# Out projection of later token tiles in groups of four with two levels of Winograd products, and where the residual stream is transposed

## The chip, the cores and the metric

The kernel runs on one core of one Trainium2 chip. The metric is the device time of one execution in microseconds (us). An execution that the hardware profiler records gives a span, from the first to the last instruction, and the device time around it. The engines are called PE (matrix products; PEld is its weight load), DVE (vector), ACT (scalar and activation), POOL (GpSimd) and SP (which here only issues DMAs). PE reads SBUF and writes PSUM; ACT and DVE read either.

## The reference, cut to what matters

Two residual blocks over 4096 tokens (64 batches of 64) of width 1024. All of it is f32 until the feed forward rounds to bf16.

```python
def reference(x, itok_B_0_15, itok_B_0_7, ...):
    # 1: a per-batch 64x64 matrix over channels, attention with 32 heads of 32, out projection
    x = x + _L0_attn_ref(_L0_cond_ref(x, itok_B_0_15, L0_cond_weights), qkvw, qkvb, ow, ob)
    # 2: dense layer with routed low-rank experts, then a quantized gated feed forward
    x = x + _L0_ffn_ref(_L0_cond2_ref(x, itok_B_0_7, W, Wr, A, B), w_gate, s_wgate, ...)
    return x
...
    def _L0_attn_ref(x, attn_qkvw, attn_qkvb, attn_ow, attn_ob):
        ...
        ctx = jnp.einsum('bhqk,bhkd->bhqd', probs, v)
        ctx = jnp.transpose(ctx, (0, 2, 1, 3)).reshape(B, S, H)
        return ctx @ attn_ow + attn_ob
```

The change is to the last line, `ctx @ attn_ow + attn_ob` and the sum with x, and to how its result, the residual stream x1, gets to the second block.

## The kernel before, in words

4096 tokens are 32 tiles of 128 rows; two tiles are a pair, so there are 16 pairs. The instructions of each engine stand in the order in which the code emits them. A tile pool hands out SBUF; a tile that takes the place of an older one waits for all uses of the older one (`reuse_waits="tile"`), whichever engine or DMA they are on.

**Attention** (`attention`) works on eight blocks of 512 tokens and writes its context, transposed, to DRAM (`ctx_d`, one tensor per pair). In the tail of the last block pairs 0 and 1 of out projection fill PE.

**Products in Winograd's form.** `Winograd` (its `product` is at L1129) computes a 256x1024 by 1024x1024 product from four quarters of each operand with seven products of quarters in place of eight. ORDER = (1, 6, 7, 5, 2, 4, 3) is the order, A_OF and B_OF name the weight and token operand of each. Four PSUM banks (`poa` to `pod`) are each used for two or more of the seven; a later product goes on summing in a bank that has been read. The weight operands A11, A12, A22 are quarters of the weight and S1 to S4 sums of quarters, made once early in the kernel and held in DRAM (`comb`). The token operands T1 to T4 are made on DVE by `sums_of_tokens` (L1139 to L1142), the context being the stationary operand and the weights the moving one (512 columns).

**Out projection** (`OutProjection`). `pair(p)` gives seven pairs of functions, `product` and `rest`. Before the first product POOL adds the bias to the two x tiles (L1250, 1024 columns each). `rest` of 1 copies the bank on ACT (`u1`, L1261), of 6 and 7 adds it on DVE to the sum before (`u6`, `u7`, L1263), and after 7 POOL adds u6 and u7 to three quarters of x (L1266, 512 columns). `rest` of 5, 2, 4 and 3 adds the bank on DVE to its quarter of x (L1269).

**The residual stream's transpose.** The second stage needs x1 with its features on the partitions. `turn` splits a half row of x1 on ACT into its low and high 16-bit planes (L1224, `xh`, 1.04 us each), has SP issue a DMA transpose of them (L1226, `xhT`), and `turned` joins the planes on ACT (L1235, `xTo`, 1.34 us each) and stores f32 to `xT_d`. That is four times per pair. SP also stores x1 itself to `out_t`, loads the context and x of the pair after next, and the second stage's base weights (one of seven per pair).

**The second stage** (`second_stage`) first runs pairs 2 to 15 of out projection, then its own 16 pairs, the last written out by hand. Three pairs are in flight (p, q = p-1, r = p-2): router and base product of p (seven products by `Winograd`, with the experts' part added in the banks), quantization and gate and up products of q, down product and result of r. `load_x1` brings the transposed x1 of the next pair (L1317), `token_sums` makes T1 to T4, `quant_a` and `quant_b` go DVE, ACT, DVE, then a DMA transpose on SP (`qT`, L1575), which the `pg` and `pu` matmuls (L1589) wait for.

## Time and profile before

| | |
|---|---|
| median of 3 runs (lowest, highest) | 2402.47 us (2402.36, 2408.15) |
| the profiled execution | 2406.19 us |
| its span, 41907 instructions | 2404.4 us |
| mean granted PE clock | 0.997 |
| out projection, pairs 2 to 15 | until 1712.0 us, where the first router matmul starts |
| second stage | 1712.0 us to the end |
| PE in it, steady state | a pair every 41.7 us (router matmuls at 1907.68 and 1949.42) |

Columns that recur below: in the groups of the page, `line engine op out<-in shapes xcount | busy us, mean ns of one | idle us before it, and what ended it`; in the timeline, `start us, length us, engine line op out<-in shapes xcount [idle before it <-releaser]`. Instructions of one engine are pipelined, so a recorded length can overlap the next start; the distance from start to start is what one costs when many stand in a row. A matmul of f32 operands leaves two records.

In out projection the slice view of the page shows PE at nine tenths or more and the DMAs at seven to eight tenths:

```profile
PE   8999999999999999999999999999999999999997
...
DVE  3573474464543644633535533324377878777787
ACT  1344344343344443443434544343333333333333
POOL 4121112111122223220000333334100000000000
PEclk9999999999999999999999999999999999999999
DMA  7899799899899998997967788877733443444353
```

Each digit is a fortieth of the span, 60.1 us; out projection ends in the 29th.

### The profile page before, as it was taken

Reading aid. Unit: us, or ns where it says so; the run is one execution under the profiler, and the core shown is the slowest. Engines: PE = TensorE matmul, PEld = TensorE weight load, DVE = VectorE, ACT = ScalarE, POOL = GpSimd, SP = SyncE. Lnnn points to the kernel's source line nnn. Section 1 sums busy time; section 2 is a strip of 40 time slices with the busy share of each in tenths; the row PEclk is TensorE's granted clock in tenths of the full one; section 3 lists DMA queues with packets and bytes.
Section 4 is the critical chain, followed back from the end, with each engine's and each line's share of the span. In section 5 each row is a group of like instructions: output and inputs, shape, how many; then the busy total and the mean of one; then the engine's idle time right before and its main releaser. Section 6 shows DMA issues by size and latency. Waiting matters only on the chain.

```text
span 2404.4 us, 41907 instructions
## 1 busy us (share of the span) xinstructions
PE 2367.6 (98%) x17066; PEld 1628.5 (68%) x17104; DVE 1334.5 (56%) x2584; ACT 936.2 (39%) x1220; POOL 418.7 (17%) x470
## 2 busy tenths in 40 slices
PE   8999999999999999999999999999999999999997
PEld 7888888888888888888888444444454545454452
DVE  3573474464543644633535533324377878777787
ACT  1344344343344443443434544343333333333333
POOL 4121112111122223220000333334100000000000
PEclk9999999999999999999999999999999999999999
DMA  7899799899899998997967788877733443444353
GB/s 229 217 240 248 190 228 241 221 232 220 208 232 274 212 255 230 242 237 179 207 188 196 213 257 258 275 218 248 239 77 75 90 79 83 84 86 82 70 119 76
DMA packets 612395, 453.84 MB, mean 189 GB/s; under 512 B 362465, under 2 KB 524258, under 8 KB 606690
## 3 DMA queue, kind: packets, MB, share of 16 engines
q1 hardware_dynamic: 581522, 393.91, 63.2%
q0 software_dynamic: 12240, 40.38, 7.9%
q10 hardware_dynamic: 18432, 16.79, 3.1%
q8 instruction: 137, 2.24, 0.4%
q14 instruction: 64, 0.52, 0.1%
HBM read 274.02 MB, written 91.23 MB: 152 GB/s over the span
## 4 chain that ended last, share of the span: by engine, by line
PE 92%; DMA 2%; DVE 1%; SPq 1%; issue 1%; ACT 0%; ACTq 0%; DVEq 0%
PE poa L1129 5%; PE poc L1129 5%; PE pod L1129 5%; PE psvc L530 4%; PE psva L530 4%; PE psvd L530 4%; PE pbc L1129 4%; PE pbd L1129 4%; PE pba L1129 4%; PE pskc L509 4%; PE pskd L509 4%; PE pska L509 4%; PE psqa L509 4%; PE psqd L509 4%; PE psqc L509 4%; PE pr L1398 2%
## 5 line engine op out<-in xcount | busy, mean ns | idle before, releaser
L582 ACT ACTIVATE prob<-prob 128x512 f32<-128x512 f32 x128 | 80.6, 629 | 346.7 <-DVE prob L578 338.6
L608 ACT COPY pT<-phT 128x1024 int16<-128x1024 int16 x128 | 165.4, 1339 | 25.4 <-DMA phT<-ph 21.4
L596 ACT COPY ph<-prob 128x1024 int16<-128x1024 int16 x128 | 133.5, 1043 | 63.1 <-DVE prob L590 38.4
L442 POOL COPY yB<-yhT 128x512 int16<-128x512 int16 (+1 forms) x84 | 75.8, 955 | 426.4 <-DMA yhT<-yh 426.4
L1636 POOL DMA_DIRECT2D out_dram<-y x29 | 25.2, 869 | 656.2 <-DVE y L1628 644.4
L577 DVE TENSOR_REDUCE mx<-s 128x8 f32<-128x512 f32 x128 | 87.4, 682 | 71.6 <-PE s L568 71.6
L1250 POOL TENSOR_TENSOR xo<-xo,ob 128x1024 f32<-128x1024 f32 x32 | 83.5, 2629 | 228.2 <-DVE prob L578 189.5
L509 PE MATMUL psqa<-yB,wq 128*128 128x256 f32 x512 | 121.1, 379 | 0.5 <-ACT psqp L479 0.5
L509 PE MATMUL pska<-yB,wk 128*128 128x256 f32 x512 | 120.9, 379 | 0.0
L1224 ACT COPY xh<-xo 128x1024 int16<-128x1024 int16 x64 | 64.4, 1041 | 142.8 <-DVE xo L1269 142.8
L530 PE MATMUL psva<-wv,yB 128*128 128x256 f32 x512 | 115.8, 379 | 0.0
L1129 PE MATMUL poa<-woA,cx 128*128 128x512 f32 x256 | 115.3, 593 | 0.0
L1129 PE MATMUL pba<-wtA,x1T 128*128 128x512 f32 x240 | 107.9, 592 | 0.0
L1235 ACT COPY xTo<-xhT 128x1024 int16<-128x1024 int16 x64 | 84.7, 1337 | 58.4 <-DMA xhT<-xh 53.3
L530 PEld LDWEIGHTS psva<-wv,yB 128*128 128x128 f32 x512 | 97.2, 190 | 14.0 <-issue 0.8
L509 PEld LDWEIGHTS psqa<-yB,wq 128*128 128x128 f32 x512 | 97.1, 190 | 14.0 <-ACT psqp L479 0.9
L509 PEld LDWEIGHTS pska<-yB,wk 128*128 128x128 f32 x512 | 97.3, 190 | 13.2
L633 ACT ACTIVATE co<-banks,bqkv 128x256 f32<-128x256 f32 x128 | 60.7, 474 | 109.3 <-PE banks L411 79.8
L1266 POOL TENSOR_TENSOR xo<-xo,ou 128x512 f32<-128x512 f32 x48 | 59.9, 1275 | 191.8 <-DVE ou L1263 191.8
L590 DVE TENSOR_TENSOR prob<-prob,den 128x512 f32<-128x512 f32 x128 | 89.4, 699 | 4.4
L578 DVE TENSOR_TENSOR prob<-s,mx 128x512 f32<-128x512 f32 x128 | 88.5, 691 | 4.5
L1129 PEld LDWEIGHTS poa<-woA,cx 128*128 128x128 f32 x256 | 48.5, 190 | 60.0 <-issue 59.5
(255 smaller groups left out, 4945.8 us busy)
## 6 DMA issues: line engine op xcount, KB each, us to landing
wv<-v_d SPq DMA_DIRECT2D x56, 512.0 KB
wq<-q_d SPq DMA_DIRECT2D x28, 1024.0 KB
wk<-k_d SPq DMA_DIRECT2D x28, 1024.0 KB
wq<-in_qkvw_dram SPq DMA_DIRECT2D x100, 256.0 KB
wk<-in_qkvw_dram SPq DMA_DIRECT2D x100, 256.0 KB
wv<-in_qkvw_dram SPq DMA_DIRECT2D x50, 512.0 KB
x<-in_x_dram SPq DMA_DIRECT2D x32, 512.0 KB
ctx_d<-co ACTq DMA_DIRECT2D x128, 128.0 KB
```

The source lines that it names most:

```text
L442: nc.gpsimd.tensor_copy(dst, src[:, :, :, halves[r] if hf else r])
L509: nc.tensor.matmul(ps[:, 0:HB], A[:, SLOT[A_OF[i]], k, :], B[B_OF[i]][:, k, :], start=first and k == 0, stop=k == KQ - 1, skip_group_check ...
L530: nc.tensor.matmul(ps[:, j * VC:(j + 1) * VC], B[B_OF[i]][:, k, j * P:(j + 1) * P], A[:, k, :], start=first and j == 0 and k == 0, stop=k ...
L577: nc.vector.tensor_reduce(mx, ps[:, :, n, :, :], AX.X, ALU.max)
L578: nc.vector.tensor_tensor(p.rearrange("p j h k -> p h j k"), ps[:, :, n, :, :], mx.unsqueeze(3).to_broadcast([P, HPC, 2, C]), ALU.subtract,)
L582: nc.scalar.activation(p, p, AF.Exp, scale=scale)
L590: nc.vector.tensor_tensor(p, p, den.unsqueeze(2).to_broadcast([P, n, C]), ALU.mult)
L596: nc.scalar.copy(h, planes(p.rearrange("p n k -> p (n k)")))
L608: nc.scalar.copy(planes(pT.rearrange("p a b q -> p (a b q)")), hT)
L1129: self.nc.tensor.matmul(ps, self.B[self.B_OF[i]][:, k, :], self.A[self.A_OF[i]][:, k, :], start=first and k == 0, stop=k == self.KQ - 1, s ...
L1235: nc.scalar.copy(planes(xT.rearrange("p k q -> p (k q)")), hT)
L1250: nc.gpsimd.tensor_add(s["x"][:, t, :], s["x"][:, t, :], self.ob)
```

## The change

Three things change together.

1. Pairs 4 to 15 become six groups of four token tiles (`OutGroups`). Each of the seven products of a group's Winograd form (the outer product) is itself computed in that form from seven products of quarters: 49 per group, each two matmuls with 256 moving columns. The second level's weight sums (S1, S2, S3 in new tiles, S4 in place of one quarter of the first level's operand) are made by DVE and POOL under pairs 2 and 3. For each outer product DVE makes four operand sums of 256 columns. Its seven products use three banks: `a` for 1, 6, 7 and 4, `b` for 5 and 3, `c` for 2. ACT copies (snapshots) bank `a` after 1, 6 and 7, into tiles with two buffers; POOL adds the snapshots, DVE adds banks `b`, `c` and the last of `a`. Each sum goes to U1, to U7 or to a quarter of x, as the first level needs, and POOL adds U1 or U7 to further quarters (`extra`). PE runs products 3 and 4 of the outer product before among those of the current one (`SEQ`). The bias is folded into U1 and U7.
2. x1's planes are stored to DRAM untransposed (`x1_d`), four plane copies on ACT per pair as before; the DMA transposes (`turned_x1`) and the joins of the planes (`joined_x1`, ACT) move into the second stage, two and two per pair, one pair ahead.
3. The second stage's base weights are loaded into the tiles of out projection's weights as each becomes free in the last group, rather than through the whole of out projection. The last pair's residual tiles are loaded as halves, the second tile's later.

The diff, cut to its core:

```diff
...
-    def turn(self, p, t):
+    def part(self, p, t):
 
         nc, n = self.tc.nc, self.H // 2
         for f in range(2):
             h = self.hp.tile([P, 2, n], I16, tag="h", name=f"xh_{p}_{t}_{f}")
             nc.scalar.copy(h, planes(self.st[p]["x"][:, t, f * n:(f + 1) * n]))
-            hT = self.hp.tile([P, 2, n], I16, tag="hT", name=f"xhT_{p}_{t}_{f}")
-            nc.sync.dma_start(
-                hT.rearrange("p h (k q) -> p (h k) q", q=P), h.rearrange("p h n -> p (h n)"), transpose=True
-            )
-            self.turning.append((p, t, f, hT))
-
-    def turned(self):
-        nc, n, KQ = self.tc.nc, self.H // 2, self.KC // 2
-        for p, t, f, hT in self.turning:
-            xT = self.hp.tile([P, KQ, P], F32, tag="xT", name=f"xTo_{p}_{t}_{f}")
-            nc.scalar.copy(planes(xT.rearrange("p k q -> p (k q)")), hT)
-            nc.sync.dma_start(self.xT_d[p][:, t, f * KQ:(f + 1) * KQ, :], xT)
-        self.turning = []
+            self.parted.append((self.x1_d[p][t, :, f, :, :], h))
+
+    def stored(self):
+        for to, h in self.parted:
+            self.tc.nc.sync.dma_start(to, h)
+        self.parted = []
 
...
+    SEQ = (("new", 1), ("old", 3), ("new", 5), ("new", 6), ("old", 4), ("new", 2), ("new", 7))
...
+    def open_right(self):
+        def pool(name, bufs):
+            return self.right.enter_context(self.tc.tile_pool(name=name, bufs=bufs, reuse_waits="tile", side="right"))
+        self.sp, self.tp, self.t2p, self.bp = pool("sg3", 1), pool("tg3", 1), pool("ug3", 2), pool("bg3", 5)
+
+    def open_left(self):
+        def pool(name, bufs):
+            return self.left.enter_context(self.tc.tile_pool(name=name, bufs=bufs, reuse_waits="tile"))
+        self.xp, self.up, self.snap = pool("xg3", 6), pool("vg3", 1), pool("ng3", 2)
+
...
+    def weight_sums(self, i):
+
+        nc, q = self.nc, self.QH
+        A = self.op.A[Winograd.A_OF[i]]
+
+        def a(m, h):
+            return A[:, 2 * h:2 * h + 2, m * q:(m + 1) * q]
+        S = self.sp.tile([P, 3, 2, q], F32, tag=f"S{i}", name=f"woS_{i}")
+        s1, s2, s3 = (S[:, n, :, :] for n in range(3))
+        self.W[i] = {"A11": a(0, 0), "A12": a(0, 1), "A22": a(1, 1), "S1": s1, "S2": s2, "S3": s3, "S4": a(1, 0)}
+        return [
+            lambda: nc.vector.tensor_tensor(s1, a(1, 0), a(1, 1), ALU.add),
+            lambda: nc.gpsimd.tensor_tensor(s3, a(0, 0), a(1, 0), ALU.subtract),
+            lambda: nc.vector.tensor_tensor(s2, s1, a(0, 0), ALU.subtract),
+        ], lambda: nc.vector.tensor_tensor(a(1, 0), a(0, 1), s2, ALU.subtract)
+
...
+    def operand_sums(self, o):
+
+        g, i = self.outers[o]
+        X = self.g[g]["B"][Winograd.B_OF[i]]
+        b = {f"B{h + 1}{t + 1}": X[:, 2 * h:2 * h + 2, t * P:(t + 1) * P] for h in range(2) for t in range(2)}
+        self.g[g]["b", i] = b
+
+        def sub(z, x, y):
+            b[z] = self.t2p.tile([P, 2, P], F32, tag=z, name=f"ug_{g}_{i}_{z}")
+            self.nc.vector.tensor_tensor(b[z], b[x], b[y], ALU.subtract)
+        return [
+            lambda: sub("T1", "B12", "B11"), lambda: sub("T2", "B22", "T1"), lambda: sub("T3", "B22", "B12"),
+            lambda: sub("T4", "B21", "T2"),
+        ]
+
...
+    def dests(self, g, i):
+
+        s = self.g[g]
+        if i in (5, 2, 4, 3):
+            T, N = {5: (1, 1), 2: (0, 0), 4: (0, 1), 3: (1, 0)}[i]
+            xd = (lambda t, n: self.x_unit(g, T, N, t, n),) * 2
+        ob = self.op.ob
+        U1 = lambda t, n: self.unit(s["U", 1], t, n)
+        return {
+            1: lambda: [(lambda t, n: ob[:, n * self.QH:(n + 1) * self.QH], U1)],
+            6: lambda: [(U1, U1)],
+            7: lambda: [(U1, lambda t, n: self.unit(s["U", 7], t, n))],
+            5: lambda: [(U1, U1), xd],
+        }.get(i, lambda: [xd])()
+
+    def add(self, o, unit, eng, what):
+
+        s, (g, i) = self.o[o], self.outers[o]
+        if i in (1, 7) and not s["begun"]:
+            self.g[g]["U", i] = self.up.tile([P, 2, self.HH], F32, tag=f"U{i}", name=f"vg_{g}_{i}")
+        for n, (src, dst) in enumerate(s["dests"]):
+            first = (n, unit) not in s["begun"]
+            s["begun"].add((n, unit))
+            eng.tensor_tensor(dst(*unit), what, (src if first else dst)(*unit), ALU.add)
+
+    def extra(self, g, i, unit):
+
+        s, gp = self.g[g], self.nc.gpsimd
+
+        def into(T, N, key):
+            x = self.x_unit(g, T, N, *unit)
+            gp.tensor_tensor(x, x, self.unit(s["U", key], *unit), ALU.add)
+
+        if i == 1:
+            into(0, 0, 1)
+        elif i == 7:
+            u = self.unit(s["U", 7], *unit)
+            c = self.HH + unit[1] * self.QH
+            gp.tensor_tensor(u, u, self.op.ob[:, c:c + self.QH], ALU.add)
+        elif i == 2:
+            into(1, 1, 7)
+        elif i == 4:
+            into(0, 1, 7)
+        elif i == 3:
+            into(1, 0, 1)
+
...
+    def product(self, o, j):
+        nc, (g, i) = self.nc, self.outers[o]
+        s = self.o[o]
+        bank = {1: "a", 6: "a", 7: "a", 4: "a", 5: "b", 3: "b", 2: "c"}[j]
+        first = bank not in s
+        if first:
+            pool, tag = (self.ps_c, "h") if bank == "c" else (self.ps_ab, "g")
+            s[bank] = pool.tile([P, 512], F32, tag=tag, name=f"pg{bank}_{g}_{i}")[:, 0:self.QH]
+        A, B = self.W[i][Winograd.A_OF[j]], self.g[g]["b", i][Winograd.B_OF[j]]
+        for k in range(2):
+            nc.tensor.matmul(
+                s[bank], B[:, k, :], A[:, k, :], start=first and k == 0, stop=k == 1, skip_group_check=True
+            )
+
+    def snapshot(self, o, j):
+        g, i = self.outers[o]
+        t = self.o[o]["s", j] = self.snap.tile([P, self.QH], F32, tag=f"s{j}", name=f"ng{j}_{g}_{i}")
+        self.nc.scalar.copy(t, self.o[o]["a"])
+
+    def after(self, o, j):
+
+        s, (g, i) = self.o[o], self.outers[o]
+        nc = self.nc
+        V, G = nc.vector, nc.gpsimd
+        if j in (1, 6, 7):
+            self.snapshot(o, j)
+        if j == 2:
+            self.add(o, (1, 0), G, s["s", 6])
+            self.add(o, (0, 0), V, s["c"])
+            self.add(o, (1, 1), V, s["b"])
+            self.add(o, (0, 0), G, s["s", 1])
+            self.extra(g, i, (0, 0))
+        elif j == 7:
+            self.add(o, (1, 1), G, s["s", 7])
+            self.extra(g, i, (1, 1))
+        elif j == 3:
+            self.add(o, (1, 0), V, s["b"])
+            self.extra(g, i, (1, 0))
+        elif j == 4:
+            self.add(o, (0, 1), V, s["a"])
+            self.extra(g, i, (0, 1))
+
...
+            for which, j in self.SEQ:
+                if which == "new" and not new or which == "old" and o == 0:
+                    continue
+                at = o if which == "new" else o - 1
+                self.product(at, j)
+                if j == 1:
+                    self.store()
+                self.after(at, j)
+                if j in (1, 6):
+                    self.part()
+                if new:
+                    if j in (1, 6) and sums:
+                        sums.pop(0)()
+                        if j == 1:
+                            sums.pop(0)()
+                    if j == 2 and sums:
+                        sums.pop(0)()
+                    if j == 2:
+                        if n == 0 and g != self.groups[0]:
+                            self.token_sum(g, 2)
+                        elif n == 2 and g != self.groups[0]:
+                            self.token_sum(g, 3)
+                        elif n == 5 and nxt:
+                            self.token_sum(nxt, 0)
+                        elif n == 6 and nxt:
+                            self.token_sum(nxt, 1)
+                    if j == 7 and n == 6 and nxt:
+                        for f in self.operand_sums(o + 1):
+                            f()
...
+        def turned_x1(p, *ns):
+
+            s = st1.setdefault(p, {"xT": {}})
+            for n in ns:
+                f, t = QUARTERS[n]
+                hT = s["hT", n] = op.hp.tile([P, 2, HH], I16, tag="h", name=f"x1h_{p}_{n}")
+                nc.sync.dma_start(
+                    hT.rearrange("p h (k q) -> p (h k) q", q=P), x1_d[p][t].rearrange("q f h n -> q f (h n)")[:, f, :],
+                    transpose=True,
+                )
+
+        def joined_x1(p, *ns):
+            s = st1[p]
+            for n in ns:
+                f, t = QUARTERS[n]
+                x = s["xT"][t, f] = xp1.tile([P, KQ, P], F32, tag="x", name=f"x1T_{p}_{n}")
+                nc.scalar.copy(planes(x.rearrange("p k q -> p (k q)")), s.pop(("hT", n)))
...
+        for p in (2, 3):
             for n, (_, product, rest) in enumerate(op.pair(p)):
                 product()
                 rest()
-            ld = next(loads_t, None)
-            if ld:
-                ld()
-            if p == NPAIR - 3:
+                for _ in range(2):
+                    if sums:
+                        sums.pop(0)()
+                if p == 2 and n >= 3:
+                    groups.load(g0, *((0, 1), (0, 0), (1, 1), (1, 0))[n - 3])
+                if p == 3:
+                    last_sums[Winograd.ORDER[n]]()
+                    if n in (1, 2, 3, 4):
+                        groups.token_sum(g0, n - 1)
+                    elif n > 4:
+                        for f in groups.operand_sums(0) if n == 5 else ():
+                            f()
+        op.stored()
+        op.stack.close()
+        ws = ctx.enter_context(tc.tile_pool(name="ws3", bufs=1, reuse_waits="tile"))
+        xp1 = ctx.enter_context(tc.tile_pool(name="x3", bufs=6, reuse_waits="tile"))
+        op.hp = ctx.enter_context(tc.tile_pool(name="hg3", bufs=2, reuse_waits="tile"))
...
+        def freed(i):
+            load_base(i)
+            if i == 1:
                 first_loads()
-        op.turned()
-        op.stack.close()
-
+            elif i == 7:
+                turned_x1(0, 0, 1)
+            elif i == 5:
+                joined_x1(0, 0, 1)
+                turned_x1(0, 2, 3)
+            elif i == 2:
+                joined_x1(0, 2, 3)
...
-            do(p > 0, load_x1, p + 1)
+            turned_x1(p + 1, 0, 1)
...
             gates_transposed(p)
+            joined_x1(p + 1, 0, 1)
+            turned_x1(p + 1, 2, 3)
...
             base(p, 4)
+            joined_x1(p + 1, 2, 3)
             after(p, 4)
...
```

## The prediction

> **What bounds the kernel now.** I read the page's busy times and chain first, then busy times by stage, then the chain in the changed stage, then the engines that the change loads.
>
> ```profile
> PE 2367.6 (98%) x17066; PEld 1628.5 (68%) x17104; DVE 1334.5 (56%) x2584; ACT 936.2 (39%) x1220; POOL 418.7 (17%) x470
> ...
> PE 92%; DMA 2%; DVE 1%; SPq 1%; issue 1%; ACT 0%; ACTq 0%; DVEq 0%
> ```
>
> PE is busy for 98% of the span and is 92% of the chain. By stage (window, length, then busy us and count of PE, PEld, DVE, ACT, POOL, then clock, DMA share, GB/s):
>
> ```profile
> 1578.00:1712.00 134.00, 134.00 (x314) 59.28 (x313) 43.52 (x54) 51.54 (x48) 49.31 (x30) 1.00 0.72 219
> 1712.00:2404.00 692.00, 672.17 (x2315) 335.51 (x2351) 533.11 (x1159) 238.25 (x314) 29.36 (x32) 0.99 0.42 94
> ```
>
> The first window is out projection (later pairs), the second the second stage. In the first PE has no gap; DVE, ACT and POOL are each busy for about a third. The chain there is PE alone:
>
> ```profile
> 1643.49 3.43 PE pob L1129 x8
> ...
> 1667.52 3.43 PE pob L1129 x8
> ```
>
> A product of four matmuls is eight records (two passes each), 3.43 us. From `pob` to `pob` is one pair, 24.03; a group of four token tiles costs 48.06 today.
>
> **Part 1, PE in six groups (pairs 4 to 15).** Per group 49 products of two 128x256 matmuls, 196 passes, replace 14 products of four 128x512, 112 passes. The price of a pass is in the Q projection:
>
> ```profile
> L509 PE MATMUL psqc<-T,wq x8: 379/379/379, 1004.2 to 1005.7; 128*128 128x256 f32 x8
> ```
>
> Seven starts in 1.5 us are 0.214 each (379 ns is the pipelined length). 196 x 0.214 = 42.0 us: 6.0 saved per group, **36 us in six**, if PE stays the bound. An outer product has 6.0 us.
>
> **Part 2, POOL.** In place of two bias adds and three adds of u per pair it gets three 256-column adds per outer product (six for i = 5, which has two targets) and four "extra" adds where a shared sum goes to a quarter. In the order of i: 7+3+7+6+7+7+7 = 44 per group. The trace has no 256-column POOL add, but has both neighbours, back to back:
>
> ```profile
> 25.86 1.27 POOL L283 TENSOR_TENSOR wk<-wk 128x512 f32<-128x512 f32 x1
> 27.09 1.26 POOL L284 TENSOR_TENSOR wk<-wk 128x512 f32<-128x512 f32 x1
> ...
> 901.68 0.46 POOL L178 TENSOR_TENSOR cs<-cs,cq 128x128 f32<-128x128 f32 x1
> 902.10 0.45 POOL L179 TENSOR_TENSOR cs<-cq 128x128 f32<-128x128 f32 x1
> 902.51 0.46 POOL L180 TENSOR_TENSOR cs<-cq,cs 128x128 f32<-128x128 f32 x1
> ```
>
> Start to start, 512 columns take 1.23 us and 128 take 0.41; the line through both gives 0.41 + 128 x 0.82/384 = 0.68 for 256 (bounds 0.41 and 1.23; I take the line). 44 x 0.68 = 30.0; eight read the result of the add just before, and such an add started 0.11 later (L282 at 24.52, L283 at 25.86): **30.9 us of 42.0**.
>
> **Part 3, DVE, and its collisions with POOL.** Per group DVE gets four token sums of 1024 columns, 28 operand sums of 256 and 32 adds from PSUM of 256. Start to start 512 columns take 0.605 (below) and 1024 take 1.14 (L363 at 17.73 and 18.87); the line gives 0.34 for 256. Own time 4 x 1.14 + 60 x 0.34 = 25.0. The first two kinds read two SBUF tiles, and those collide with POOL today:
>
> ```profile
> 1655.52 0.69 DVE L1140 TENSOR_TENSOR To<-cx,To 128x512 f32<-128x512 f32 x1
> 1656.13 0.68 DVE L1141 TENSOR_TENSOR To<-cx 128x512 f32<-128x512 f32 x1
> 1656.73 2.84 DVE L1142 TENSOR_TENSOR To<-cx,To 128x512 f32<-128x512 f32 x1
> 1659.49 0.68 DVE L1269 TENSOR_TENSOR xo<-poa,xo 128x512 f32<-128x512 f32 x1
> ```
> ```profile
> 1656.34 5.45 POOL L1250 TENSOR_TENSOR xo<-xo,ob 128x1024 f32<-128x1024 f32 x2 [1.40 <-issue]
> ```
>
> L1142 takes 2.84 instead of L1140's 0.69: it stood until POOL's first add was through. POOL's two adds took 5.45 instead of 2 x 2.35 (L282 to L284 with 1024 columns): 0.75 lost to 0.39 left of L1141 and 0.605 of L1142, so POOL pays three quarters of such a DVE time. L1269, which reads PSUM, ran undisturbed beside POOL's second add.
>
> Per group DVE holds POOL up for 0.75 x (28 x 0.34 + 4 x 1.14 = 14.1) = 10.6: POOL's line is **41.5**, DVE's 25.0 + 32 waits of some 0.4 = 38, PE's 42.0. Two lines almost equal to PE's leave no room where work bunches. It does at a group's end: DVE has a token sum and six operand sums in a row (3.2 us), each alternating with one of the five adds that POOL then has ready (3.4). From its last PSUM add, at 5.95 of the outer product, that brings it to 12.5, where the next PSUM add was due at 7.8. POOL's last two extra adds follow that, to 14.3; U1 has one buffer, so DVE's first add of the new group waits for them, its second ends at 15.1, and the product that goes on in that bank was to start at 12.9. PE stands about 2.2 there and 0.3 for the first operand sums: 2.5 at each of five ends, and I add 0.5 per group elsewhere. 6 x 42.5 + 5 x 2.5 = 267.5 against 288.4: **-21**. Bounds: no stall, 252, -36; and every add paying 0.11, full blocking and gaps of 2, 30.0 + 4.8 + 14.1 + 2 = 51, +17.
>
> The Trainium skill ("SBUF — State Buffer", Who interferes with whom) says that whichever of the two starts first holds the shared ports for its whole instruction and the other fully blocks. DVE's wait agrees, POOL's three quarters doesn't quite; by the rule POOL's line would be 45.0 and set the pace, and the sum would end near 2402, no gain.
>
> ACT gets 21 snapshots at 0.37 (L479, 128x256) and eight plane copies at 1.04: 16 us of 42, no bound.
>
> **Part 4, pairs 2 and 3.** Products stay; 28 sums of the weights go under them, 7 on POOL at 1.23 and 21 on DVE at 0.605. POOL: 16.8 + 8.6 + 1.2 for the bias half, 26.7, plus 0.75 x 21 of two-tile sums on DVE: 42 of 48. DVE: 28.4 and some 16 of waits, 45 of 48. Hidden, though pair 3 is the denser: 0 to 4, **+1**.
>
> **Part 5, seams.** The groups' x tiles and snapshots take the room of pair 3's tiles: SP loads x after pair 3's stores, and the first snapshots wait for the plane stores that ACT (2.1 us of copies) and SP still have to make; PE needs those snapshots two products later. Bounds 0 to 8, **+3**. In the last group the first pair's joins (2 x 2.7 on ACT) wait for transposes issued on SP behind 1 MB weight loads, snapshots queued behind: 0 to 4, **+1**. After it eight plane copies (8.3 us) stand on ACT before the second stage's first copy, whose bank PE needs five products later: 0 to 5, **+1**.
>
> **Part 6, second stage.** Four 1.34 us joins (L1235 today) per pair and their transposes move here. ACT is 34% busy; the question is place. Two joins go between these:
>
> ```profile
> 1928.98 0.37 ACT L1460 COPY gT<-ghp 128x256 f32<-128x256 f32 x1 [7.41 <-PE ghp L1458]
> 1929.25 1.15 ACT L1562 ACTIVATE q_g<-q_g,rs_g 128x1024 f32<-128x1024 f32 x1
> ```
>
> q_g goes 2.7 later. DVE's clip of it, at 1933.96, stands 0.3; DVE has 1.5 idle at 1941. The transpose issued at 1934.41 is needed by `pg` at 1941.67. On SP two transposes (1.23 to issue) replace a 0.4 load and two more wait for the joins, qT's transpose 0.1 late behind them. Nothing reaches PE: **+1**, bounds 0 and 15 (1 us per pair); with no cover 5.4 per pair, 80. The joins, transposes and stores removed from out projection were under PE: nothing gained.
>
> **Sum.** -21 + 1 + 3 + 1 + 1 + 1 = -14. The profiled execution took 2406.2 (span 2404.4, 1.8 around it), so 2392; the median of the runs is 3.7 below it: **2389 us**.
>
> **Rivals.**
> *PE alone.* DVE and POOL mesh, PE never waits: 2402.5 - 36 + 4, about 2370. For it: PSUM and snapshots are buffered over two outer products. Against: the group ends above.
> *POOL and DVE set the pace (other side).* Each add meets a wait: collisions cost POOL the full DVE time and dependent starts are the rule. From a group of 47 us on the gain is gone with the seams; at 50, 6 x 2 + 7: about 2421. For it: both lines are within 10% of PE's, in order, and feed each other. Against: DVE sums that fall where POOL waits cost nothing.
> *The second stage pays.* The joins reach PE with 1 us per pair: 2389 + 14, about 2403. For it: DVE is 77% busy and in order there. Against: the slack counted above.
>
> **How the numbers follow.** Forecast 0.48, PE alone 0.22, POOL and DVE 0.16, second stage 0.08, a mixture or a seam 0.06. A measurement of this kernel can tell 0.3%, 7 us, from no change: faster is below 2395. The forecast's own range, 2378 to 2399, puts 0.36 there and 0.12 in the same; PE alone all 0.22; the second stage 0.05 same and 0.03 slower; the rest 0.02, 0.03, 0.01. Faster 0.60, same 0.20, slower 0.20. The range goes from PE alone, 2369, to a group of 49: 6 x 1 + 6 above 2402, 2414.
>
> **What would show it.** In the groups: PE busy 90 to 97% with gaps at the group ends released by DVE; POOL's 256-column adds at 0.73, some near 1.1; operand sums on DVE at 0.42 or near 1; a group every 44 to 46 us. The second stage stays at 692 within a few us. I am wrong if a group takes over 48, if PE waits there for ACT or DMA first, or if POOL is busy for much under 70%.

## The result, and the profile after

The changed kernel takes **2420.28 us** (median of 4 runs, 2417.98 to 2423.63); the kernel before, on the same chip, 2403.82 (4 runs, 2402.36 to 2408.15). The ratio is 1.0063, 95% interval [1.0048, 1.0078]: slower by 0.6%, where 2389 and "faster" were forecast. The profiled execution took 2421.44 us, its span is 2419.6, 15.2 longer than before.

The page of the changed kernel, busy times and chain:

```profile
PE 2348.3 (97%) x17608; PEld 1726.7 (71%) x17608; DVE 1486.3 (61%) x2869; ACT 969.5 (40%) x1334; POOL 549.1 (23%) x682
...
PE 89%; DVE 4%; DMA 3%; SPq 1%; ACT 1%; issue 1%; POOL 0%; ACTq 0%; DVEq 0%; POOLq 0%
```

PE is busy for 19 us less than before and yet the end is later: it stands still somewhere. Busy times by stage of the changed kernel show where: six rows for the six groups, the last one for the second stage's beginning (columns as before: window, length, busy us and count of PE, PEld, DVE, ACT, POOL, then granted clock, DMA share, GB/s).

```profile
1423.20:1472.20 49.00, 44.04 (x189) 37.47 (x188) 34.40 (x65) 11.44 (x24) 29.92 (x38) 0.93 0.40 151
1472.20:1516.30 44.10, 43.00 (x198) 36.93 (x198) 37.39 (x66) 15.48 (x29) 38.04 (x45) 1.00 0.57 191
1516.30:1560.35 44.05, 42.94 (x197) 36.91 (x196) 37.36 (x65) 15.48 (x29) 37.97 (x45) 1.00 0.57 192
1560.35:1604.78 44.43, 43.17 (x197) 36.92 (x196) 37.33 (x65) 15.42 (x29) 37.99 (x45) 1.00 0.57 190
1604.78:1648.85 44.07, 42.96 (x198) 36.92 (x197) 37.39 (x65) 15.43 (x29) 38.02 (x45) 1.00 0.57 191
1648.85:1707.50 58.65, 50.09 (x205) 41.57 (x204) 34.35 (x65) 21.87 (x36) 37.72 (x48) 0.91 0.73 219
1707.50:1746.00 38.50, 20.71 (x68) 10.90 (x67) 8.64 (x32) 9.16 (x13) 4.10 (x6) 0.78 0.96 316
```

The four middle groups are as short as forecast: 44.05 to 44.43 us against 48.06. The first group takes 49.0, the last 58.65, and in the row after them PE is busy for 20.7 of 38.5 us. Those are also the rows with a clock under 1.

The chain of waits through the last group and into the second stage names what held the end back (start, us, what):

```profile
1662.96 1.08 SPq L1576
1664.09 0.94 SPq L1577
1665.07 3.89 SPq L1579
1669.01 0.60 SPq L1579
1670.75 5.92 DMA x_d<-xh
1676.75 0.93 ACT xh L1451
1677.82 4.31 DMA x_d<-xh
1682.15 2.15 SPq L1563
1684.39 6.32 DMA x1h<-x_d
1691.07 1.31 ACT x1T L1573
1692.93 3.78 PE pga L1413 x8
...
1706.06 2.00 ACT xh L1451 x2
1708.10 6.08 DMA x_d<-xh
...
1723.57 4.58 DMA bm<-in_b_t_dram
1728.28 1.26 POOL bmd L1665
...
1732.15 5.90 PE pbb L1129 x8
```

For 30 us, 1662.96 to 1692.93, PE is not on it. SP issues `awr` and `lang_i` (L1576 to L1579); the store of a plane, issued at 1670.75, stands behind them; ACT's next plane copy needs that store's buffer; PE's snapshot stands behind the copy (a stall of 4.09 us). Then the turning load and its join do the same (3.36 us). After the last group come plane stores, then `bm`, then POOL's `bmd`, then PE: a stall of 17.33 us at 1732.15. The links between `bmd` and PE, in the timeline (POOL twice, then DVE):

```profile
1728.28 1.26 POOL L1665 TENSOR_TENSOR bmd<-bm 128x512 f32<-128x512 f32 x1 [17.96 <-DMA bm<-in_b_t_dram]
1729.50 0.14 POOL L1670 IOTA ei<- 128x8 int32 x1
1729.67 0.17 DVE L1672 CAST ef<-ei 128x8 f32<-128x8 int32 x1 [21.30 <-POOL ei L1670]
```

DVE's first token sums (`T`, from 1730.62), which PE waits for, stand behind `ef`.

### The profile page after: what moved, and what is told of

Same layout as the page of the kernel before. It is cut to its first block, busy times and chain, and to the rows that moved or that the text cites. A ratio compares the mean times of both kernels' runs of the same rounds, so it can differ in the third digit from the quotient of the medians.

```text
span 2419.6 us, 43734 instructions
## 1 busy us (share of the span) xinstructions
PE 2348.3 (97%) x17608; PEld 1726.7 (71%) x17608; DVE 1486.3 (61%) x2869; ACT 969.5 (40%) x1334; POOL 549.1 (23%) x682
## 4 chain that ended last, share of the span: by engine, by line
PE 89%; DVE 4%; DMA 3%; SPq 1%; ACT 1%; issue 1%; POOL 0%; ACTq 0%; DVEq 0%; POOLq 0%
PE psvc L530 5%; PE psva L530 5%; PE psvd L530 5%; PE pga L1413 4%; PE pskd L509 4%; PE pskc L509 4%; PE pbc L1129 4%; PE pbd L1129 4%; PE psqa L509 4%; PE pska L509 4%; PE pba L1129 4%; PE psqd L509 4%; PE psqc L509 4%; PE pr L1695 2%; PE psvb L530 2%; PE pgb L1413 2%
## 5 line engine op out<-in xcount | busy, mean ns | idle before, releaser
L1413 PE MATMUL pga<-woS,ug_T 128*128 128x256 f32 x432 | 111.6, 391 | 10.5 <-ACT ng L1420 10.5
L1420 ACT COPY ng<-pga 128x256 f32<-128x256 f32 x126 | 46.8, 372 | 166.2 <-PE pga L1413 160.0
L1413 PEld LDWEIGHTS pga<-woS,ug_T 128*128 128x128 f32 x432 | 83.5, 195 | 24.7 <-ACT ng L1420 12.2
L544 DVE TENSOR_TENSOR vals<-psvd,psvu 64x256 f32<-64x256 f32 (+1 forms) x96 | 40.6, 422 | 76.6 <-PE psvd L530 75.6
L588 DVE TENSOR_REDUCE den<-prob 128x8 f32<-128x512 f32 x128 | 86.4, 675 | 0.0
L1573 ACT COPY x1T<-x1h 128x1024 int16<-128x1024 int16 x64 | 80.9, 1331 | 5.6 <-DMA x1h<-x_d 5.6
```

Of the source, the lines that this page charges most:

```text
L588: nc.vector.tensor_reduce(den, p, AX.X, ALU.add)
L1413: nc.tensor.matmul(s[bank], B[:, k, :], A[:, k, :], start=first and k == 0, stop=k == 1, skip_group_check=True)
L1573: nc.scalar.copy(planes(x.rearrange("p k q -> p (k q)")), s.pop(("hT", n)))
```

## The experiments

The profiled executions, one per kernel, begin the first group anywhere between 1416.8 and 1425.9 us, for reasons of the work ahead of pair 2: pairs 2 and 3 themselves take 48.2 to 48.3 us in all. So beside the medians I use one **stretch** of that one execution: from the first group's first product (before: pair 4's) to the first base product of the second stage's second pair. Behind it all kernels need the same time: 656.6 us before, 656.5 in the changed kernel, 656.0 to 657.1 in the others. The runs were made on several chips; each ratio is to the kernel before on the same chip.

One group of one execution is not exact: the last groups of the change and of e1, whose code is the same, differ by 3.6 us. What an edit did is therefore read from the wait that it aims at first, and from the lengths second.

| kernel | median us (ratio to before) | first group | middle four | last | second stage's start | stretch |
|---|---|---|---|---|---|---|
| before | 2403.82 | | | | 35.8 | 324.2 |
| the change | 2420.28 (1.0063) | 49.0 | 176.6 | 58.7 | 55.6 | 339.9 |
| no_extras | one run, 2415.72 | 48.3 | 173.2 | 55.8 | 57.5 | 334.8 |
| e1 | 2411.05 (1.0043 [1.0026, 1.0060]) | 47.7 | 176.9 | 55.1 | 51.6 | 331.3 |
| e2 | 2406.67 (1.0014 [1.0002, 1.0027]) | 49.0 | 176.9 | 52.3 | 49.4 | 327.6 |
| e3 | 2405.65 (1.0015 [1.0005, 1.0026]) | 48.7 | 176.7 | 51.7 | 50.2 | 327.2 |
| e4 | 2399.12 (0.9984 [0.9974, 0.9994]) | 47.2 | 176.2 | 46.6 | 49.3 | 319.3 |
| e5 | 2398.09 (0.9980 [0.9969, 0.9991]) | 47.7 | 177.0 | 46.7 | 47.9 | 319.3 |
| e6a | 2394.81 (0.9961 [0.9946, 0.9975]) | 42.8 | 176.3 | 46.5 | 47.6 | 313.2 |
| e6 | 2387.94 (0.9938 [0.9918, 0.9958]) | 42.8 | 173.1 | 45.5 | 48.1 | 309.4 |
| e7 | 2387.91 (0.9940 [0.9922, 0.9959]) | 46.2 | 172.3 | 45.0 | 44.3 | 307.8 |
| e8 | 2384.41 (0.9914 [0.9898, 0.9929]) | 46.2 | 172.3 | 45.0 | 38.7 | 302.2 |
| e9 | **2380.14** (0.9911 [0.9895, 0.9928]) | 42.8 | 172.5 | 45.6 | 38.9 | 299.7 |

**e1: POOL's order at the second stage's start.**

```diff
-        nc.gpsimd.tensor_tensor(bmd, bm[:, hs[0]], bm[:, hs[1]], ALU.subtract)
 ...
         nc.vector.tensor_scalar(bias, bias, LANG_BIAS, None, ALU.mult)
+        nc.gpsimd.tensor_tensor(bmd, bm[:, hs[0]], bm[:, hs[1]], ALU.subtract)
```

> The changed kernel with one instruction of the second stage's setup moved: POOL's subtraction bmd, which waits for the load of bm, is issued after ei, ef, rank and bias instead of before them. Nothing is added or left out. Theory A (the 17.3 us in which PE stands still after the last group are a queue of POOL: ei stands behind bmd, bmd waits for bm, bm's load stands on SP behind the plane stores, and DVE's token sums stand behind ef): the idle falls from 17.3 us to under 3, the slow matmuls behind it go too, and the time falls by 17 to 20 us, to 2400 to 2403. Rival B (DVE's token sums would have been late in any case, because ACT's joins and its eight plane copies at the end of the last group are late, and the POOL queue only overlaps with that): the time falls by under 6 us and the wait is named after ACT or a DMA.

The stall named in A is gone from PE's waits between the last group and the second pair, yet only 4.0 us of the start were won (55.6 to 51.6; the rest of e1's 8.6 is in the first and last groups, which the edit doesn't touch), and the median is above A's range. PE's waits of e1 there (who waited for whom, us in total, times, longest):

```profile
PE pr L1695 <- ACT x1T L1573: 4.9, 2, 3.2
PE ghp L1755 <- DVE gh L1742: 2.7, 1, 2.7
PE pbd L1760 <- DMA bm<-in_b_t_dram: 1.9, 1, 1.9
```

PE now meets `bm` itself, DVE's routing work (`gh`) and, for the second pair, the joins of planes whose turning loads are late. A is right on the mechanism and wrong on the size; B's wait by ACT was there, but behind the POOL queue and hidden by it.

**e2 and e3: two stalls of the last group, one at a time.** e2 is e1 with

```diff
-            if i == 1:
-                first_loads()
-            elif i == 7:
+            if i == 7:
 ...
+        first_loads()
         groups.run(freed)
```

> e1, and the loads of awr and lang_i, which SP issues inside the last group, are issued before the first group instead. Theory A (the 4.1 us stall of PE in the last group is ACT waiting for an h buffer whose store SP issued late, because the 6.5 us of issuing awr and lang_i stood before it): the stall in the middle of the last group falls under 1 us, and with the slow matmuls behind it the time is 5 to 8 us under e1. Rival B (the store's own transfer beside the 1 MB weight loads is what makes the buffer late, whoever is ahead of it on SP): the last group keeps its length within 2 us and the time is that of e1 within 2 us.

In e2 the first stall fell from 3.87 (e1) to 0.28 us, the second grew from 1.86 to 3.83: the last group is 2.8 us shorter and the stretch 3.7, not 5 to 8. A's cause is shown; part of the gain went into the next wait. e3 is e1 with the joins later:

```diff
-            elif i == 5:
+            elif i == 2:
                 joined_x1(0, 0, 1)
                 turned_x1(0, 2, 3)
-            elif i == 2:
+            elif i == 3:
                 joined_x1(0, 2, 3)
```

> e1, and in the last group the four joins of the second stage's first planes come one old product later each (the first two with product 2, the other two with product 3; the second turning loads with product 2). Theory A (the 3.4 us stall of PE near the end of the last group is a snapshot standing on ACT behind a join that waits 5 us for its turning load): the stall is gone and the last group is 3 to 6 us shorter, the time 3 to 6 us under e1. Rival B (the turning loads are late by as much again, and the wait goes along with the joins to the second stage's start): the group is shorter, but PE waits by as much before the second stage's first products, and the time is that of e1 within 2 us.

The second stall is gone (1.87 us in e1), the first is still 3.71; the last group is 3.4 us shorter, the stretch 4.1, the median 5.4: A.

**e4: all seams together.** The own edits of e2 and e3, three instead of two weight sums behind each product of pairs 2 and 3, and `bm` loaded within the last group. e1's move of `bmd` is left out here and in all that follow; with `bm` early, `ei` no longer waits for it:

```diff
-                for _ in range(2):
+                for _ in range(3):
 ...
         def freed(i):
             load_base(i)
-            if i == 1:
-                first_loads()
+            if i == 4:
+                bm = sep["bm"] = op.wp.tile([P, H], F32, tag="ob", name="bm")
+                nc.sync.dma_start(bm, a["b_t"].rearrange("e r o -> (e r) o"))
```

> All of it together: awr and lang_i before the first group, the joins one old product later, bm loaded in the last group (with product 4) instead of after it, and three instead of two weight sums behind each product of pairs 2 and 3, so that DVE and POOL have them behind them in pair 3. Theory A (the loss against the prediction lies at the seams, and the steady groups are as short as forecast): first group 45 to 47 us, last group 44 to 47, PE idle under 3 us at the start of the second stage; time 2383 to 2392, faster than the kernel before. Rival B (the engines' work at the seams, 20 plane copies and joins on ACT and 28 weight sums beside the groups, does not fit whatever the order; a wait removed comes back as another): time 2396 to 2404, no faster than before.

The groups came about as A has them (47.2, 46.6); the time, 2399, is B's: a wait removed did come back. The stall of 17.3 us is down to 1.0 with `bmd` still ahead of `ei`. The second stage's start still took 49.3 us, with PE waiting 6.7 and 1.8 us for the second pair's joins.

**e5, e8: the second pair's turning loads.** e5 is e4 with

```diff
+        turned_x1(1, 0, 1)
         ig = load_row("ig", a["inv_gate"], H)
 ...
-            turned_x1(p + 1, 0, 1)
+            if p:
+                turned_x1(p + 1, 0, 1)
```

> The kernel with the seams mended (e4), and SP issues the first two turning loads of the second stage's second pair of planes before the nine loads of scales and weights of the second stage (about 5 MB) instead of behind them. Theory A (the 6.7 and 1.8 us for which PE waits for the joins of that pair, and the slow matmuls after each, are the turning loads standing on SP and in the DMA queue behind those nine loads): the wait falls under 2 us, the second stage's second router product begins 7 us earlier against its first, and the time is 7 to 11 us under that of e4, 2388 to 2392. Rival B (the turning loads need the h buffers, which the last plane copies hold until about then, so issuing them sooner only lets SP wait and the nine loads start later): within 2 us of e4, or the wait for scales and weights takes its place.

The second router product did begin 6.2 us earlier against the first (34.7 instead of 40.9), and the time stayed within 2 us of e4, which is B's number, but for another reason than B's: the wait went from the first and second turning load to the third and fourth. Timeline of e5, SP first, then PE:

```profile
1711.26 2.92 SPq L1563 DMA_TRANSPOSE x1h<-x_d  x2
...
1721.64 11.90 SPq L1563 DMA_TRANSPOSE x1h<-x_d  x2
```
```profile
1728.23 1.09 PE L1699 MATMUL pr<-awr,x1T 128*128 128x136 f32 x8
1736.11 5.54 PE L1699 MATMUL pr<-awr,x1T 128*128 128x136 f32 x24 [6.79 <-ACT x1T L1573]
```

Two turning loads ahead of the nine loads were issued in 2.9 us, two behind them in 11.9. That plane buffers are not what they wait for, as B has it, is seen in e7: a third buffer leaves the wait at 6.4 us. e8 (on top of e7, below) moves seven of the nine behind these two as well; `late_loads` holds `wg`, `wu`, `wd` and their scales:

```diff
             joined_x1(p + 1, 0, 1)
             turned_x1(p + 1, 2, 3)
+            if p == 0:
+                late_loads()
```

> e7, and the second stage's weights and scales that its first quantized products need only a pair later (wg, wu, wd and four rows of scales, about 4.5 MB) are loaded behind the third and fourth turning load of the second pair of planes instead of ahead of them. Theory A (in e5 to e7 the wait of 6.4 to 6.8 us before the second router product is this third turning load, standing about 9 to 10 us behind those loads; e5 moved only the first two turning loads ahead, so the wait went on to the next two): the wait is gone, the slow matmuls behind it too, time 2378 to 2382. Rival B (the weights are then late for the first quantized products, some 35 us on, and PE waits there for them instead): within 2 us of e7's 2388.

The wait and the slow matmuls are gone: 38.7 us at the second stage's start, 5.6 less, and no new wait for weights (one of 2.6 for DVE's first token sums is left). The median, 2384.4, is above A's range; the six runs go from 2377 to 2389, and in the profiled one the work ahead of the groups ended 7.3 us later than in e7's.

**e6 and e6a: DVE at the groups' ends and at their beginning.** e6a puts off four in-place sums of pair 3 into the first group; e6 also spreads the operand sums:

```diff
-                sums = self.operand_sums(o + 1) if n + 1 < 7 else []
+                sums = self.operand_sums(o + 1) if o + 1 < len(self.outers) else []
 ...
-                    if j == 7 and n == 6 and nxt:
-                        for f in self.operand_sums(o + 1):
-                            f()
+                    if j == 2 and g == self.groups[0] and n < 4:
+                        self.late[n]()
```

> e5, with less of DVE's work at the groups' seams: the last four of pair 3's in-place weight sums are put off into the first group, where the first two token sums of the other groups leave room; and the four operand sums for a group's first outer product are spread over the step before it, as everywhere else, instead of standing behind a token sum at its end. Theory A (the stalls of 0.5 and 0.6 us at each group's end, and the 0.6 us one in the first group, are DVE late behind a token sum of 1.5 to 1.7 us; and the first group's 2.9 us stall is ACT's plane copies late behind DVE's last adds of pair 3): steady groups 43.0 to 43.6 us instead of 44.1, first group 2 to 4 us shorter, time 5 to 9 us under e5. Rival B (POOL, busy 38 of 44 us, sets the steady groups' pace as soon as DVE doesn't, and the first group waits for POOL or ACT): steady groups still 44 us, time within 3 us of e5.

> e5 with only the first half of e6: the last four in-place weight sums are put off into the first group; the operand sums at the groups' ends stay where the change has them. Theory A (the two halves are separate: this one shortens the first group, the other one takes 1.0 us from every group's end): steady groups 44.0 to 44.4 us, as in the changed kernel; first group 43 to 45 us; time 2390 to 2395. Rival B (the gain of e6 lies in the groups' ends alone, or in the chip): first group over 46 us and a time within 2 us of e5's 2398.

Both go A's way, e6 with a little more than expected (10.2 us under e5). e6a took 5.0 us from the first group and left the middle ones; the spreading took 3.2 from the middle four. This is the order at a group's end that e6 undid, in the changed kernel (timeline, DVE, then PE):

```profile
1516.30 1.46 DVE L1333 TENSOR_TENSOR tg_T<-cg,tg_T 128x1024 f32<-128x1024 f32 x1
1517.68 0.94 DVE L1344 TENSOR_TENSOR ug_T<-cg 128x256 f32<-128x256 f32 x1
```
```profile
1518.68 1.13 PE L1413 MATMUL pgb<-woS,ug_T 128*128 128x256 f32 x4 [0.50 <-DVE ug_T L1344]
```

The product needs the operand sum `ug_T`, which stands behind a token sum `tg_T`.

**e7 and e9: how many buffers for planes.** e7 is e6 with three, e9 is e8 with two again:

```diff
-        op.hp = ctx.enter_context(tc.tile_pool(name="hg3", bufs=2, reuse_waits="tile"))
+        op.hp = ctx.enter_context(tc.tile_pool(name="hg3", bufs=3, reuse_waits="tile"))
```

> e6 with three buffers for planes instead of two in the groups and the second stage. Theory A (with two buffers ACT's plane copies of the last group, and the turning loads that share the buffers, stand behind each other's transfers): ACT's idle time before the plane copies falls by half, the last group is 1 to 3 us shorter, time 1 to 5 us under e6. Rival B (with the seams mended no plane copy's wait reaches PE): within 1.5 us of e6.

> e8 with two buffers for planes again, as in e6. Theory A (the third buffer of e7 gained nothing because it moved the groups' snapshots into room whose last plane store lands later: the first group's stall is 3.3 us in e7 and e8 and 1.5 in e6, while the last group is only 0.5 us shorter): first group near 43 us instead of 46.2, last group 45 to 46, stretch from the first group to the second router's first base product 298 to 301 us (302.2 in e8), time 2378 to 2383. Rival B (the first group's length comes from pair 3's last adds, whatever the buffers): first group again 46 us, time that of e8 or 1 to 3 us above it.

e7 gained nothing in time, but not because no wait was left: ACT's idle time before the plane copies did halve (10.4 to 4.6 us from the last group on), and the second stage's start fell by 3.8 us, but the first group rose by 3.5. There the group's first snapshot now waited for the landing of a plane store (`x_d`), in e6 only the second one; that the pools' moved room is the cause is inferred from that releaser. e9 keeps the good side of both, and was as A says in all four numbers. It is faster than the kernel before by 0.9%, and than the change by 40 us (by the medians; the stretches differ by as much, 40.2).

**no_extras: what POOL's load costs.** 

```diff
+        return
         if i == 1:
             into(0, 0, 1)
```

> The changed kernel with POOL's 20 further adds per group left out (the sums of units 1 and 7 into the residual stream's other quarters and the last bias): POOL has 24 instead of 44 adds of 256 columns in a group. Theory A (PE's 196 passes set the steady groups, and what is over them is DVE behind a token sum at the group's end): POOL busy falls to about 21 us of a group, steady groups stay 43.5 to 44.2 us, time within 4 us of the changed kernel. Rival B (POOL's line, with DVE's holds, sets part of the pace): steady groups fall to 42.5 us or less, and the time by 8 us or more.

```profile
1514.02:1557.32 43.30, 42.62 (x197) 37.03 (x196) 33.60 (x65) 15.39 (x29) 19.59 (x25) 1.00 0.57 195
```

The view is that of the stages, for one middle group. These take 43.30 us each, between the two expectations: with 20 adds fewer, POOL's busy time halves and the group gains 0.85 us. PE's wait of 0.60 us for DVE's `vg` is gone at the group's end, the one for `ug_T` stays (0.7 us). So POOL doesn't set the pace, but through DVE it costs the group's end a part of its stall.

## Why the prediction was wrong

The spans differ by 15.2 us. It adds up so, with the middle groups' 44.15 as the measure of a steady group:

| step | forecast us | measured us |
|---|---|---|
| Parts 1 to 3, six steady groups | -21 | 6 x 44.15 - 288.4 = -23.5 |
| work ahead of pair 2, not part of the change | 0 | 1375.05 - 1375.42 = -0.4 |
| Part 4, pairs 2 and 3 (what ran over is in the first group) | +1 | 48.17 - 48.18 = 0.0 |
| Part 5, first group | +3 | 49.0 - 44.15 = +4.9 |
| Part 5, last group | +1 | 58.65 - 44.15 = +14.5 |
| Part 5, after the last group, with Part 6's beginning | +1 | 55.6 - 35.8 = +19.8 |
| Part 6, steady second stage | +1 | -0.1 |

*Part 1* was right: a pass takes 0.216 us start to start, forecast 0.214; at 42.3 us for 196 passes some 34 of the 36 us were to be had.

*Part 2* was right: POOL's 256-column adds follow each other at about 0.70 where nothing holds them (three in 2.13 us), forecast 0.68 (timeline):

```profile
1701.31 1.41 POOL L1388 TENSOR_TENSOR xg<-xg,vg 128x256 f32<-128x256 f32 x2
...
1708.18 2.13 POOL L1388 TENSOR_TENSOR xg<-xg,vg 128x256 f32<-128x256 f32 x3
```

*Part 3* had the mechanism right and the collisions too dear. POOL is busy for 38.0 us of a middle group instead of 41.5, since DVE holds it up by some 7 us (38.0 less the forecast's 30.9 for its own adds), not 10.6; DVE's 37.4 was forecast as 38. Where one group follows another there is the stall, released by DVE, but 1.1 us of it instead of 2.5: 0.5 for `ug_T` and 0.6 for `vg`, whose add on DVE had itself waited 1.0 us for POOL's last extra adds, as foreseen. The rule of the Trainium skill ("SBUF — State Buffer", Who interferes with whom), that whoever holds the shared ports blocks the other fully, would have put POOL's line at 45.0; the measured 38.0 speaks against taking it as a full sum of both. The holds go both ways: in no_extras DVE's own busy time falls from 37.4 to 33.6, 0.19 us per add left out.

*Part 5* is the step that failed. It forecast +5 for three seams, and they took 39.2. What it said: "wait for transposes issued on SP behind 1 MB weight loads, snapshots queued behind", 0 to 4, and "eight plane copies (8.3 us) stand on ACT before the second stage's first copy", 0 to 5. It followed ACT's queue alone, and priced each wait by itself. Two of the signs of being wrong came true there and only there: groups of over 48 us (49.0 and 58.65), and PE's longest waits released by ACT.

- In the last group the snapshots did queue behind the joins on ACT (the 3.36 us stall, e3). But SP carries the plane stores too, and the stores stood behind `awr` and `lang_i` (the 4.09 us stall, e2). `lang_i` alone kept SP for 4.53 us; its two loads took 3.61 before, where nothing on SP was urgent.
- At the second stage's start PE stood behind a queue of POOL, and that behind ACT's copies: the diff moves the load of `bm` behind the last plane stores, `bmd` waits for it, and `ei`, which the whole setup on DVE and the first token sums need, is the next instruction of POOL. The trace of before has a pair of lines that bears on it (timeline, POOL):

```profile
1708.81 1.27 POOL L1368 TENSOR_TENSOR bmd<-bm 128x512 f32<-128x512 f32 x1 [5.78 <-PE poc L1129]
1710.03 0.14 POOL L1373 IOTA ei<- 128x8 int32 x1
```

  There `bmd` waits for an out projection tile's room and not for `bm`, which SP had issued at 1684.56, 24 us ahead. In the changed kernel SP issues it at 1723.57, behind the last plane store. The eight plane copies ahead of that took 16.6 us (1706.06 to 1722.68), twice the 8.3 forecast: ACT's timeline has three waits among them, of 6.20, 1.25 and 1.18 us, for the landing of a store that holds the buffer.
- Behind that queue stood two more waits that the 17.3 us covered: the turning loads of the second pair behind nine loads (e1, e5, e8). The prediction costed the turning loads in the steady second stage (+1, right) and not at its start, where before one plain load of `x1T` had been issued ahead of the nine.
- In the first group the forecast +3 was nearly right in size (4.9), and the snapshots did stand behind plane copies on ACT (the 2.94 us stall). But what made the copies late was DVE, with work that Part 4 had called hidden: pairs 2 and 3 took no longer, but the last in-place sum starts 4.6 us after the group's first product (1423.22), and PE's first operand sum stands in the same queue (timeline; PE, DVE, ACT, PE):

```profile
1426.27 1.13 PE L1413 MATMUL pgb<-woS,ug_T 128*128 128x256 f32 x4 [2.02 <-DVE ug_T L1344]
1427.86 0.68 DVE L1317 TENSOR_TENSOR woS<-woS,woS 128x512 f32<-128x512 f32 x1
1428.02 1.99 ACT L1220 COPY xh<-xo 128x1024 int16<-128x1024 int16 x2 [1.62 <-DVE xo L1257]
1430.33 2.07 PE L1413 MATMUL pga<-woS,ug_T 128*128 128x256 f32 x4 [2.94 <-ACT ng L1420]
```

  With the weight sums done sooner (e4) the first of these stalls fell to 0.60 us; with four of the in-place sums put off (e6a) it is gone and the second is 1.46.

*The clock* is a term the sum didn't have. After each of the longer stalls PE ran at half speed for a few us; the second stall of the last group, on PE's timeline:

```profile
1692.93 2.07 PE L1413 MATMUL pga<-woS,ug_T 128*128 128x256 f32 x4 [3.36 <-ACT ng L1420]
1694.80 1.91 PE L1413 MATMUL pga<-woA,ug_T 128*128 128x256 f32 x4
1696.51 1.91 PE L1413 MATMUL pgc<-woA,tg_T 128*128 128x256 f32 x4
1698.21 1.45 PE L1413 MATMUL pga<-woS,ug_T 128*128 128x256 f32 x4
1699.50 1.03 PE L1413 MATMUL pga<-woS,cg 128*128 128x256 f32 x4
```

Four products from 1692.93 to 1699.50 take 6.57 us instead of 4 x 0.865: 3.1 lost on top of 3.36. The same count gives 3.0 after the first group's 2.94 us stall, 1.8 after the 4.09 and 2.3 after the 17.33, 10.2 us in all, a quarter of what the seams cost. The Trainium skill ("TensorE: Matmul & The Clock Gate", Part 1) has the clock fall to half after an idle window of about 3.4 us, and says that the window runs freely. These runs agree that idle time costs the clock, and that a stall's length alone doesn't decide it, but less than 3.4 us was enough: stalls of 1.46 and 2.28 us (e9) cost no clock, 2.94, 3.36 and 4.09 did, and one of 2.04 (e1) did where another of 2.02 didn't.

*The rivals.* "POOL and DVE set the pace" named 2421 and the time is 2420, but its condition, groups of 50 us, isn't what happened; the middle groups never took over 44.5, and the agreement is luck. The mechanism on the other side, seams in SP's and POOL's queues, was left to 0.06 for "a mixture or a seam". That the seams put the time outside the range, and not the groups' own work, is shown by e6 and e9: with the same products, adds and planes in another order they take 2387.9 and 2380.1 us, inside the range and below the 2389 forecast. That e6 comes within 1.1 us of it is luck too: its middle groups, at 43.3 us, are shorter than the 42.5 + 2.5 of Part 3.

## What to carry to other kernels

A change that shortens a steady loop has to be costed at its first and last pass, by walking each in-order queue, SP and POOL too, from the moved load to whoever stands behind the instruction that waits for it. Where several waits end close together, removing the latest only shows the next: here the first edits returned 4.0 us of a stall of 17.3 (e1) and next to nothing of one of 6.7 (e5), until the weight loads ahead of the last turning loads were moved too (e8). In this kernel a stall of some 3 us or more in a dense stream on PE cost a further 1.8 to 3.1 us of half clock.

## What was not expected of the hardware

- Two turning loads issued behind nine loads of about 5 MB kept SP's queue for 11.9 us, against 2.9 ahead of them (e5) and 2.6 in most pairs of the changed kernel's steady second stage.
- DVE and POOL hold each other up in both directions, by about 0.19 us per POOL add for DVE (37.4 against 33.6 us with 20 adds fewer, no_extras) and some 7 us per group for POOL, half of the 14.1 us that DVE's sums of two SBUF tiles take by the prediction's count.
- A third buffer for planes lengthened a stall over 40 us ahead of the first plane copied into that pool (at 1466.3 in e7): the first group's was 3.27 us with three (e7) and 1.46 with two (e6, e9).
